# The chosen block's heads with values as the standing operand, and late weight loads one behind each routed tile

## The chip, the cores and the metric

The kernel runs on one core of a Trainium2 chip. The metric is device time in microseconds (us) of one execution. The engines are named as the profile names them: PE multiplies matrices (PEld loads its weights), DVE and ACT do element-wise work, POOL is GpSimd, SP issues DMAs. All arithmetic is fp32; in the trace every fp32 matmul shows as two records.

## The reference, cut to what matters

The input is 2 x 2048 tokens of 256 features. Two layers follow each other. Layer 0 adds a causal attention (one head of 256) and a mixture of 8 experts (each token goes to its two best experts, and two shared experts see all tokens). Layer 1 adds another causal attention and a second feed-forward part that treats only the 255 best-scored tokens of each 2048, the "chosen block":

```python
hn = rmsnorm(x_sel, ln1)                       # 255 chosen tokens
q, kk = rope(heads(hn @ wq)), rope(heads(hn @ wk))
v = heads(hn @ wv)                             # 16 heads of 16
sc = einsum('bhqd,bhkd->bhqk', q, kk) / 4 + m_sel
a = softmax(sc)
o = einsum('bhqk,bhkd->bqhd', a, v).reshape(b, kc, d) @ wo
x1 = x_sel + o
x2 = x1 + gelu(rmsnorm(x1, ln2) @ w1) @ w2     # w1: 256 x 1024
```

The change touches two places: how `einsum(a, v)` of the chosen block is formed, and when weights for later stages are loaded during the routed experts.

## The kernel before, in words

Four stages follow each other on PE. First layer 0's attention (to about 355 us). Then the routed experts (about 355 to 736 us): `for t in range(LIKELY)` runs 36 tiles of 256 sorted tokens, each by `run(t)`. A tile loads the three weights of its expert (`rw`, 512 KB each) and the biases on SP's queue (line 682, 686; two buffers each), fetches its tokens by a transposing DMA (L691), makes fp32 of them on POOL (L696), multiplies gate and up (L703), applies Silu on ACT (L711), multiplies with up on DVE (L712), multiplies down (L718), adds the bias on DVE (L723) and stores (L724). Third the shared experts (L1312, L1331), and fourth layer 1's attention (scores L251, values L316, and L1361 for its queries).

Work that is not in the main chain stands in generators in a list, `side`; `beside()` advances them by a credit after each piece of main work. `chosen_block(b)` is such a generator. For the first half of the tokens (b = 0) its heads run beside the shared experts, about 1059 to 1145 us, and its feed-forward part to 1175 us; for the second half (b = 1) it runs beside layer 1's attention, its heads about 1370 to 1452 us. A scheduler then orders the instructions of each engine's queue, so that the place in a queue differs from the place in the text.

The 16 heads of the chosen block are treated in pairs `h`, and the 256 queries in halves `r`: 16 units for each b. A unit passes three functions, one step apart, so that three units are under way:

- `weigh(h, r)`: queries of the two heads masked on DVE (L1152), two 256-column matmuls for the scores (L1157), scale and mask on DVE (L1162), the maximum (L1167), Exp on ACT with the row's sum (L1170), the reciprocal of the sum (L1173).
- `cross`: four 128 x 128 transposes of the softmax rows on PE (L1179), evacuated to `prT` by DVE or ACT in turn (L150, L152).
- `gather`: four matmuls (L1191) with a 128 x 128 block of `prT` as the standing weights and 16 columns of values `vs` moving; DVE multiplies by the reciprocal into `o` (L1195).

After the 16 units, `o` is transposed (L995), multiplied with `f_wo` (L1222), added to x (L1226), normalised (`rmsnorm`, L1007 to L1015), transposed again and passed to the feed-forward matmuls (L1237) with Gelu on ACT (L1242). These PSUM results all use one tag, `mm`, of two banks.

The late weights are those that the shared experts and layer 1 need. `later_weights()` (L637) issues 17 loads in one go on ACT's queue: eight of 256 KB, six of 512 KB, and three small ones. In the text it is called after tile 18. `layer1_products` multiplies four of them with each other after tile 24 (eight 256-column matmuls).

Of the kernel before, what the change touches and what calls it, by code (L numbers as in the profile page):

```python
# [9 lines left out]
F32 = mybir.dt.float32  # L10
# [3 lines left out]
AF = mybir.ActivationFunctionType  # L14
# [3 lines left out]
P = 128  # L18
# [28 lines left out]
def transformer_kernel(ctx: ExitStack, tc: tile.TileContext, a: dict, out: bass.AP):  # L47
# [15 lines left out]
    def bank(tag):  # L63
        return psum.tile([P, 512], F32, tag=tag, name=f"ps_{tag}")
# [81 lines left out]
    def evacuate(dst, src):  # L146

        copies[0] += 1
        if copies[0] % 2:
            nc.vector.tensor_copy(dst, src)  # L150
        else:
            nc.scalar.copy(dst, src)  # L152
# [17 lines left out]
    def weight(pool, name, tag, queue=None, cols=None):  # L170

        k, n = a[name].shape
        t = pool.tile([P, k // P, cols or n], F32, tag=tag, name=tag)
        (queue or nc.scalar).dma_start(t[:, :, :n], a[name].rearrange("(c p) n -> p c n", p=P))
        return t
# [461 lines left out]
    def later_weights():  # L637

        for n in ("f_wq", "f_wk", "f_wv", "f_wo"):
            fw[n] = weight(w1pool, n, n)  # L640
        for n in ("wq1", "wk1", "wv1", "wo1T"):
            raw[n] = weight(raw_pool, n, n)
        nc.scalar.dma_start(wvo[:, :, D:], a["router_w"].rearrange("(c p) n -> p c n", p=P))
        for n in range(2):
            for name, k in (("sw1", 2), ("sw2", 2), ("sw3", 4)):
                w[name, n] = shared_pool.tile([P, k, 2 * H // k], F32, tag=f"{name}{n}", name=f"{name}{n}")
                nc.scalar.dma_start(w[name, n], a[name][n].rearrange("(c p) n -> p c n", p=P))
        for k, name in enumerate(("sb1", "sb2")):
            w[name] = shared_pool.tile([P, 8], F32, tag=name, name=name)
            nc.scalar.dma_start(w[name], a[name])  # L650

    def layer1_products(after):

# [16 lines left out]
    with ExitStack() as moe:  # L670
        hp = moe.enter_context(tc.tile_pool(name="routed", bufs=2))

        def run(t):
# [24 lines left out]
            for h in range(0, 4, 2):  # L698
                p1, p2 = bank("sc"), bank("tr")
                for ps, we_in in ((p1, w1), (p2, w2)):  # L700
                    for k in range(2):
                        for dc in range(2):
                            nc.tensor.matmul(  # L703
                                ps[:, k * TT : (k + 1) * TT],
                                lhsT=we_in[:, dc, (h + k) * P : (h + k + 1) * P], rhs=xT[:, dc, :],
                                start=(dc == 0), stop=(dc == 1),
                            )
                for k in range(2):
                    act = hp.tile([P, TT], F32, tag="act", name="act", bufs=3)
                    at, hc = slice(k * TT, (k + 1) * TT), slice(h + k, h + k + 1)  # L710
                    nc.scalar.activation(act, p1[:, at], AF.Silu, bias=b1[:, hc])  # L711
                    nc.vector.scalar_tensor_tensor(  # L712
                        hid[:, h + k, :], p2[:, at], b2[:, hc], act, op0=ALU.add, op1=ALU.mult
                    )
# [7 lines left out]
            y = hp.tile([P, 2, D], F32, tag="y", name="y", bufs=3)  # L722
            nc.vector.tensor_tensor(y, po, b3.unsqueeze(1).to_broadcast([P, 2, D]), ALU.add)  # L723
            nc.sync.dma_start(sorted_y[part, :].rearrange("(r p) d -> p r d", p=P), y)  # L724
            return product

        for t in range(LIKELY):
            product = run(t)
            if t == LIKELY // 2:
                later_weights()  # L730
            if t == LIKELY // 2 + 6:
                layer1_products(product)
        used = nc.values_load(filled[0:1, 0:1], min_val=0, max_val=NT)
        with tc.If(used > LIKELY):
            for t in range(LIKELY, NT):
# [237 lines left out]
    def chosen_block(b, fp):  # L973
# [164 lines left out]
        nc.vector.memset(mask[:, :, TOPK - 1 :], -3.0e38)  # L1138
        yield

        o = fp.tile([P, 2, D], F32, tag="hn", name="o")
        queries = {}

        def weigh(h, r):

            dc = h // 8
            if r == 0:

                queries[h] = fp.tile([P, 2, TOPK], F32, tag="qm", name="qm", bufs=2)
                for k in range(2):  # L1150
                    m = (h + k) % 8
                    nc.vector.tensor_scalar(  # L1152
                        queries[h][:, k, :], qkT[:, dc, :], head_of[:, m : m + 1], None, op0=ALU.mult
                    )
            ps = bank("mm")
            for k in range(2):
                nc.tensor.matmul(  # L1157
                    ps[:, k * TOPK : (k + 1) * TOPK], lhsT=queries[h][:, k, r * P : (r + 1) * P],
                    rhs=qkT[:, 2 + dc, :], start=True, stop=True,
                )  # L1160
            pr = fp.tile([P, 2, TOPK], F32, tag="pr", name="pr", bufs=2)
            nc.vector.scalar_tensor_tensor(  # L1162
                pr, ps.rearrange("p (k n) -> p k n", k=2), 0.25,
                mask[:, r, :].unsqueeze(1).to_broadcast([P, 2, TOPK]), op0=ALU.mult, op1=ALU.add,
            )
            nmx = small.tile([P, 2], F32, tag="f_nmx", name="f_nmx")
            nc.vector.tensor_reduce(nmx, pr, AX.X, ALU.max, negate=True)  # L1167
            total = small.tile([P, 2], F32, tag="f_total", name="f_total")
            for k in range(2):
                nc.scalar.activation(  # L1170
                    pr[:, k, :], pr[:, k, :], AF.Exp, bias=nmx[:, k : k + 1], accum_out=total[:, k : k + 1]
                )
            nc.vector.reciprocal(total, total)  # L1173
            return h, r, pr, total

        def cross(h, r, pr, total):
            ps = bank("mm")
            for k in range(4):
                nc.tensor.transpose(  # L1179
                    ps[:, k * P : (k + 1) * P], pr[:, k // 2, (k % 2) * P : (k % 2 + 1) * P], ident  # L1180
                )
            prT = fp.tile([P, 512], F32, tag="prT", name="prT", bufs=2)
            evacuate(prT, ps)
            return h, r, prT, total

        def gather(h, r, prT, total):
            po = bank("mm")
            for k in range(2):
                for c in range(2):
                    at = (2 * k + c) * P  # L1190
                    nc.tensor.matmul(  # L1191
                        po[:, k * HD : (k + 1) * HD], lhsT=prT[:, at : at + P],
                        rhs=vs[:, c, (h + k) * HD : (h + k + 1) * HD], start=(c == 0), stop=(c == 1),
                    )
            nc.vector.tensor_tensor(  # L1195
                o[:, r, h * HD : (h + 2) * HD].rearrange("p (k d) -> p k d", k=2),
                po[:, : 2 * HD].rearrange("p (k d) -> p k d", k=2),
                total.unsqueeze(2).to_broadcast([P, 2, HD]),
                ALU.mult,
            )  # L1200


        first = second = None
# [8 lines left out]
            first = weigh(*unit) if unit else None  # L1212
            yield

        oT = fp.tile([P, 2, TOPK], F32, tag="hT", name="oT")
        transposed(o, oT)
        yield
        x1 = fp.tile([P, 2, D], F32, tag="x1", name="x1")
        for r in range(2):
# [225 lines left out]
```

## Time and profile before

| what | value |
|---|---|
| median of 3 runs | 1566.82 us (1565.46 to 1573.57) |
| profiled execution | 1565.43 us |
| its span in the trace, and mean granted clock | 1563.7 us, 0.984 |
| PE busy, share of the span | 1485.9 us, 95% |
| DVE, ACT, POOL busy | 693.1, 449.5, 408.4 us |
| DMA moved | 183.51 MB, mean 117 GB/s |

PE is busy for 95% of the span; the other engines for less than half. The profiled execution lies 1.4 us below the median, and 1.7 us above its own span. Every duration in this document up to the result is of this execution.

### The profile page before, as it was taken

The page shows a single profiled execution, that of the slowest core. Times are in us where ns is not written, and L with a number is a line of the kernel's source. Part 1 is how long each engine was busy: PE and PEld are TensorE (multiplying, and loading weights), DVE is VectorE, ACT ScalarE, POOL GpSimd, SP SyncE. Part 2 cuts the span into 40 slices and gives each one's busy share as a digit, 9 for nine tenths or more (in the row PEclk, how much of TensorE's full clock was granted, in tenths as well). Part 3 has the DMA queues.
Part 4 walks back from the last instruction along what each step waited for, and adds up shares of the span by engine and source line. Part 5 has one row for each costly group of instructions (what it writes and reads, how often), then busy time and mean ns, then how long its engine had stood idle before and what let it go on. Part 6 is the DMA issues. An engine that isn't in the chain of part 4 may idle for free.

```text
span 1563.7 us, 18180 instructions
## 1 busy us (share of the span) xinstructions
PE 1485.9 (95%) x5956; PEld 1059.9 (68%) x5956; DVE 693.1 (44%) x2067; ACT 449.5 (29%) x838; POOL 408.4 (26%) x594
## 2 busy tenths in 40 slices
PE   6999899997999999999999999999989998998998
PEld 4666566666888888888556556566665765676665
DVE  6346333341222222222234446766545468665354
ACT  2443333331111111111121221125624433343233
POOL 3555577531111111110111111122003123411132
PEclk9999999999999999999999999999999999998999
DMA  5844665669878888674010110220005435521144
GB/s 158 252 112 106 152 135 135 154 127 244 238 219 214 216 216 215 197 207 127 28 41 27 41 41 31 70 90 27 1 10 114 104 75 121 130 49 22 28 118 101
DMA packets 290559, 183.51 MB, mean 117 GB/s; under 512 B 192960, under 2 KB 265408, under 8 KB 290464
## 3 DMA queue, kind: packets, MB, share of 16 engines
q1 hardware_dynamic: 255168, 134.95, 35.5%
q10 hardware_dynamic: 27664, 26.53, 5.8%
q0 software_dynamic: 7632, 20.86, 4.3%
q8 instruction: 48, 0.79, 0.2%
q14 instruction: 47, 0.39, 0.1%
HBM read 93.14 MB, written 45.14 MB: 88 GB/s over the span
## 4 chain that ended last, share of the span: by engine, by line
PE 32%; issue 9%; DVE 6%; POOL 3%; DMA 2%; ACT 1%; POOLq 0%; ACTq 0%; DVEq 0%
PE ps_tr L1312 6%; PE ps_sc L1312 6%; PE ps_pv L1331 5%; POOL planes L301 3%; PE ps_mm L1191 2%; PE ps_mm L1157 2%; PE ps_pv L316 2%; DMA across<-planes 1%; PE ps_sc L251 1%; DVE x L1342 1%; PE ps_mm L1237 1%; PE ps_mm L1179 1%; PE ps_tr L251 1%; PE ps_mm L794 1%; PE ps_mm L1249 1%
## 5 line engine op out<-in xcount | busy, mean ns | idle before, releaser
L301 POOL COPY planes<-row 128x512 uint16<-128x512 uint16 (+3 forms) x320 | 167.5, 568 | 313.6 <-ACT row L270 300.9
L282 ACT COPY pT<-across 128x512 uint16<-128x512 uint16 (+3 forms) x160 | 106.1, 677 | 222.9 <-DMA across<-planes 212.6
L251 PE MATMUL ps_sc<-xnT,qT 128*128 128x512 f32 (+3 forms) x384 | 161.4, 541 | 1.4 <-ACT qT L152 1.2
L712 DVE SCALAR_TENSOR_TENSOR hid<-ps_tr,be,act 128x256 f32<-128x256 f32 x144 | 63.1, 480 | 204.1 <-PE ps_tr L703 187.8
L711 ACT ACTIVATE act<-ps_sc,be 128x256 f32<-128x256 f32 x144 | 60.4, 471 | 310.0 <-PE ps_sc L703 294.1
L1301 POOL DMA_INDIRECT ya<-sorted_y,place x64 | 62.2, 972 | 320.7 <-DVE x L1342 221.3
L718 PE MATMUL ps_pv<-rw,hid 128*128 128x256 f32 x576 | 134.1, 386 | 5.8 <-DVE hid L712 5.8
L316 PE MATMUL ps_pv<-vg,pT 128*128 128x256 f32 x544 | 126.1, 384 | 13.1 <-ACT pT L282 12.7
L703 PE MATMUL ps_sc<-xT,rw 128*128 128x256 f32 x576 | 136.2, 379 | 1.6 <-POOL xT L696 1.6
L703 PE MATMUL ps_tr<-xT,rw 128*128 128x256 f32 x576 | 136.1, 379 | 0.0
L316 PE MATMUL ps_pv<-v,pT 128*128 128x256 f32 x544 | 128.6, 382 | 5.2 <-ACT pT L282 4.1
L696 POOL COPY xT<-xs 128x512 uint16<-128x512 uint16 x72 | 51.5, 762 | 307.5 <-issue 273.1
L316 PEld LDWEIGHTS ps_pv<-vg,pT 128*128 128x128 f32 x544 | 102.6, 191 | 37.5 <-ACT pT L282 18.2
L718 PEld LDWEIGHTS ps_pv<-rw,hid 128*128 128x128 f32 x576 | 106.2, 192 | 27.9 <-DVE hid L712 12.9
L1312 PE MATMUL ps_tr<-xnT,sw 128*128 128x512 f32 x256 | 122.4, 594 | 0.0
L1312 PE MATMUL ps_sc<-xnT,sw 128*128 128x512 f32 x256 | 122.1, 596 | 0.1
L703 PEld LDWEIGHTS ps_sc<-xT,rw 128*128 128x128 f32 x576 | 109.4, 190 | 16.8 <-POOL xT L696 2.0
L703 PEld LDWEIGHTS ps_tr<-xT,rw 128*128 128x128 f32 x576 | 109.4, 190 | 14.9
L316 PEld LDWEIGHTS ps_pv<-v,pT 128*128 128x128 f32 x544 | 101.0, 189 | 27.1 <-ACT pT L282 8.1
L1331 PE MATMUL ps_pv<-sw,hid 128*128 128x256 f32 x512 | 118.6, 381 | 0.0
L1331 PEld LDWEIGHTS ps_pv<-sw,hid 128*128 128x128 f32 x512 | 95.9, 190 | 18.0 <-issue 5.7
L281 DVE COPY pT<-across 128x512 uint16<-128x512 uint16 (+3 forms) x160 | 69.0, 437 | 85.0 <-DMA across<-planes 84.3
(316 smaller groups left out, 1964.9 us busy)
## 6 DMA issues: line engine op xcount, KB each, us to landing
rw<-in_rw SPq DMA_DIRECT2D x108, 512.0 KB, 4.4
sorted_x<-zero ACTq DMA_DIRECT2D x13, 768.0 KB, 6.6
sorted_y<-y SPq DMA_DIRECT2D x36, 256.0 KB, 5.0
be<-biases SPq DMA_DIRECT2D x36, 132.0 KB, 4.5
table<-xn SPq DMA_DIRECT2D x8, 514.0 KB, 3.5
x<-in_x SPq DMA_DIRECT2D x8, 512.0 KB, 6.7
gains<-zero ACTq DMA_DIRECT2D x8, 512.0 KB, 3.2
gain<-gains SPq DMA_DIRECT2D x16, 256.0 KB, 2.7
```

Of the source, the lines that this page charges most:

```text
L251: product = nc.tensor.matmul(ps[:, :w], lhsT=qT[:, dc, (i % 4) * P : (i % 4 + 1) * P], rhs=xnT[g0 + k][:, dc, :w], start=(dc == 0), stop=( ...
L281: nc.vector.tensor_copy(words[:, :, 1], flat[:, :w]),
L282: nc.scalar.copy(words[:, :, 0], flat[:, w : 2 * w]),
L301: nc.gpsimd.tensor_copy(planes[:, h * w : (h + 1) * w], halves[:, :, 1 - h])
L316: product = nc.tensor.matmul(pv[:, :D], lhsT=turned[k][:, j : j + P], rhs=values[g0 + k][:, j // P, :D], start=(c + j == 0), stop=(c + j = ...
L703: nc.tensor.matmul(ps[:, k * TT : (k + 1) * TT], lhsT=we_in[:, dc, (h + k) * P : (h + k + 1) * P], rhs=xT[:, dc, :], start=(dc == 0), stop ...
L711: nc.scalar.activation(act, p1[:, at], AF.Silu, bias=b1[:, hc])
L712: nc.vector.scalar_tensor_tensor(hid[:, h + k, :], p2[:, at], b2[:, hc], act, op0=ALU.add, op1=ALU.mult)
L718: product = nc.tensor.matmul(po[:, r, :], lhsT=hid[:, hc, r * P : (r + 1) * P], rhs=w3[:, hc, :], start=(hc == 0), stop=(hc == 3),)
L1301: nc.gpsimd.indirect_dma_start(out=ya, out_offset=None, in_=sorted_y, in_offset=bass.IndirectOffsetOnAxis(ap=place[rank][:, t : t + 1], ax ...
L1312: product = nc.tensor.matmul(ps, lhsT=ww[:, dc, hc * P : (hc + 1) * P], rhs=xnT[g][:, dc, :], start=(dc == 0), stop=(dc == 1),)
L1331: product = nc.tensor.matmul(po[:, :D], lhsT=hid[:, hc, j * P : (j + 1) * P], rhs=w["sw3", n][:, hc, :], start=(hc == 0), stop=(hc == 3),)
```

## The change

It has two parts that do not touch each other.

In the heads, `gather` does nothing for `r == 0` and works once for each pair of heads, over all 256 queries. The values of one head are copied by DVE into a field of zeros, `apart`, at a fixed place; a 128-column window of it, shifted by the head's place, is the standing operand, so that the head's 16 columns stand at their own rows of the result and the rest is zero. The softmax rows, kept for both halves in `wide`, move as 256 columns. Four such matmuls (2 heads x 2 blocks of keys) accumulate in one bank, and DVE adds the bank to `oT`, which is thereby already transposed. The sums are kept for all heads, and the normalisation is made once at the end: one reciprocal, a copy that spreads each sum over 16 columns, four transposes, and one product.

In the routed experts, `later_weights` becomes a generator that names one load at a time; from tile 12 on, one load is issued behind each tile, with an order dependency on the tile's last Silu. `layer1_products` moves from tile 24 to tile 28.

```diff
     def later_weights():
         for n in ("f_wq", "f_wk", "f_wv", "f_wo"):
-            fw[n] = weight(w1pool, n, n)
+            fw[n] = w1pool.tile([P, 2, D], F32, tag=n, name=n)
+            yield fw[n], a[n].rearrange("(c p) n -> p c n", p=P)
...
-                    nc.scalar.activation(act, p1[:, at], AF.Silu, bias=b1[:, hc])
+                    activated = nc.scalar.activation(act, p1[:, at], AF.Silu, bias=b1[:, hc])
...
+        coming = later_weights()
         for t in range(LIKELY):
-            product = run(t)
-            if t == LIKELY // 2:
-                later_weights()
-            if t == LIKELY // 2 + 6:
+            product, activated = run(t)
+            if t >= LIKELY // 3:
+                for dst, src in (next(coming, (None, None)),):
+                    if dst is not None:
+                        i = nc.scalar.dma_start(dst, src)
+                        tc.add_manual_dep(i.ins, activated.ins.name, order, reason="behind a tile")
+            if t == LIKELY - 8:
                 layer1_products(product)
...
-        o = fp.tile([P, 2, D], F32, tag="hn", name="o")
+        wide = fp.tile([P, 2, 2, 2, TOPK], F32, tag="big", name="wide")
+        gap = P - HD
+        apart = fp.tile([P, 2, 2, 2 * gap + HD], F32, tag="apart", name="apart")
+        nc.gpsimd.memset(apart, 0.0)
+        total = fp.tile([P, 2, HEADS], F32, tag="total", name="total")
+        oT = fp.tile([P, 2, TOPK], F32, tag="hn", name="oT")
...
-            nc.vector.reciprocal(total, total)
-            return h, r, pr, total
+            return h, r, pr
...
-            evacuate(prT, ps)
-            return h, r, prT, total
+            evacuate(
+                wide[:, h // 2 % 2, :, :, r * P : (r + 1) * P], ps.rearrange("p (k c n) -> p k c n", k=2, c=2)
+            )
+            return h, r
-        def gather(h, r, prT, total):
+        def gather(h, r):
+            if r == 0:
+                return
+            dc, at = h // 8, h % 8 * HD
             po = bank("mm")
             for k in range(2):
+                nc.vector.tensor_copy(apart[:, k, :, gap : gap + HD], vs[:, :, (h + k) * HD : (h + k + 1) * HD])
                 for c in range(2):
-                    at = (2 * k + c) * P
+                    lo = gap - at - k * HD
                     nc.tensor.matmul(
-                        po[:, k * HD : (k + 1) * HD], lhsT=prT[:, at : at + P],
-                        rhs=vs[:, c, (h + k) * HD : (h + k + 1) * HD], start=(c == 0), stop=(c == 1),
+                        po[:, :TOPK], lhsT=apart[:, k, c, lo : lo + P], rhs=wide[:, h // 2 % 2, k, c, :],
+                        start=(k + c == 0), stop=(k + c == 2),
                     )
-            nc.vector.tensor_tensor(
-                o[:, r, h * HD : (h + 2) * HD].rearrange("p (k d) -> p k d", k=2),
-                po[:, : 2 * HD].rearrange("p (k d) -> p k d", k=2),
-                total.unsqueeze(2).to_broadcast([P, 2, HD]),
-                ALU.mult,
-            )
+            if at == 0:
+                nc.vector.tensor_copy(oT[:, dc, :], po[:, :TOPK])
+            else:
+                nc.vector.tensor_add(oT[:, dc, :], po[:, :TOPK], oT[:, dc, :])
...
-        oT = fp.tile([P, 2, TOPK], F32, tag="hT", name="oT")
-        transposed(o, oT)
+        nc.vector.reciprocal(total, total)
+        sums = fp.tile([P, 2, D], F32, tag="hT", name="sums")
+        nc.vector.tensor_copy(
+            sums.rearrange("p r (h n) -> p r h n", n=HD), total.unsqueeze(3).to_broadcast([P, 2, HEADS, HD])
+        )
+        ps = bank("mm")
+        for dc in range(2):
+            for r in range(2):
+                at = (2 * dc + r) * P
+                nc.tensor.transpose(ps[:, at : at + P], sums[:, r, dc * P : (dc + 1) * P], ident)
+        nc.vector.tensor_tensor(oT, ps.rearrange("p (c n) -> p c n", c=2), oT, ALU.mult)
```

In the built program the change also alters the order of the queues. ACT's queue before has the 17 loads ahead of and among the Silus of the first routed tiles; after, one load stands behind every fourth Silu from the 52nd on. On PE, the main work's matmuls stand at other places among those of the chosen block: five shared-expert gate and up matmuls of 512 columns (2.5 pairs) stand after the `f_wo` product of b = 0, with 16 down matmuls of 256 columns behind them; and 13 of the attention's value matmuls (L316) stand among the last five head units of b = 1, where before there were none.

## The prediction

> **What bounds the kernel now.** I read the page first, for the engine that fills the span and for the slices in which it doesn't:
>
> ```profile
> span 1563.7 us, 18180 instructions
> PE 1485.9 (95%) x5956; PEld 1059.9 (68%) x5956; DVE 693.1 (44%) x2067; ACT 449.5 (29%) x838; POOL 408.4 (26%) x594
> ...
> PE   6999899997999999999999999999989998998998
> ...
> PEclk9999999999999999999999999999999999998999
> ```
>
> PE bounds it. Each digit is 39 us; a change can gain only by removing PE work, or by filling the few slices below 9. So I asked for busy times by stretch, around the places that the diff touches (columns: length, then PE, PEld, DVE, ACT, POOL busy with counts, clock, DMA share, GB/s):
>
> ```profile
> 376.00:386.00 10.00, 5.38 (x17) 4.50 (x18) 1.57 (x3) 0.84 (x2) 0.00 (x0) 0.66 1.06 365
> 396.00:736.00 340.00, 339.85 (x1568) 293.56 (x1567) 79.40 (x163) 55.31 (x132) 43.04 (x60) 1.00 0.76 207
> 1040.00:1150.00 110.00, 108.86 (x504) 76.31 (x502) 65.83 (x163) 59.32 (x109) 11.85 (x12) 1.00 0.05 15
> 1150.00:1175.00 25.00, 20.50 (x76) 15.60 (x76) 6.70 (x37) 2.39 (x4) 1.97 (x2) 0.86 0.03 11
> 1427.00:1460.00 33.00, 25.64 (x97) 18.06 (x97) 10.69 (x26) 7.81 (x23) 0.00 (x0) 0.69 0.00 1
> ```
>
> Three holes stand out, each with a lowered clock: early in the routed stage, after the heads of b = 0, and in the last head units of b = 1. The rest of the routed stage is full to 0.15 us in 340. PE's waits in those stretches name the causes:
>
> ```profile
> PE ps_pv L718 <- DVE hid L712: 5.7, 1, 5.7
> ...
> PE ps_mm L995 <- DVE hn L1015: 4.6, 1, 4.6
> ...
> PE ps_mm L1179 <- ACT pr L1170: 6.3, 4, 1.6
> ```
>
> **Part B, the late loads.** The scheduler has put the 17 loads at the start of the routed stage, 354.9 to 386 us, not at tile 18. The timeline there:
>
> ```profile
> 371.55 7.93 ACTq L647 DMA_DIRECT2D sw<-in_sw  x2
> ...
> 379.57 0.84 ACT L711 ACTIVATE act<-ps_sc,be 128x256 f32<-128x256 f32 x2 [8.11 <-DMA sw<-in_sw]
> 380.08 0.88 DVE L712 SCALAR_TENSOR_TENSOR hid<-ps_tr,be,act 128x256 f32<-128x256 f32 x2 [8.07 <-ACT act L711]
> ...
> 380.62 4.16 PEld L718 LDWEIGHTS ps_pv<-rw,hid 128*128 128x128 f32 x12 [6.07 <-DVE hid L712]
> 380.62 4.56 PE L718 MATMUL ps_pv<-rw,hid 128*128 128x256 f32 x12 [5.67 <-DVE hid L712]
> ```
>
> ACT sits behind its own DMA issues for 8.11 us; the Silu is late, so `hid` is, so PE stands for 5.67 us. Then twelve records at the lowered clock take 4.56 us; at full clock eight records of this shape take 1.73 us from start to start, 0.216 each, so twelve take 2.6. Loss: 5.7 + (4.6 - 2.6 = 2.0), less about 0.4 for the drained end: 7.3 us.
>
> After the change one issue stands behind a tile's last Silu. An issue takes 0.37 to 0.49 us on ACT, and ACT is idle 2.6 to 6.1 us between its pairs of Silus in the steady stage: nothing, and without that cover at most 17 x 0.45 = 8 us. What else the loads need is DMA time. A tile lasts 10.4 us at a share of 0.76; 512 KB more at the 365 GB/s of the burst are 1.4 us of a tile, raising the share to about 0.9. The stretch from 386 to 396 us ran at 1.13 with PE busy for 10.00 of 10, so SP's `rw` loads (4.4 us to land, double-buffered against 10.4) should keep up; they pass on another queue. Bounds for contention: 0, and, if each of the six 512 KB loads delayed its tile by the 2.6 us by which burst loads grew (`rw` landed in 7.0 there), 16 us. I take 0, by the stretch at 1.13. The eight matmuls of `layer1_products` (8 x 0.43 us) only move by four tiles. **B: -7.3 us.**
>
> **Part A, PE work.** For a pair of heads there were two groups of L1191, eight records each. Undisturbed, a group takes 0.81 to 0.92 us from its start to the next matmul's (1059.14 to 1059.95; 1064.85 to 1065.77), 1.62 to 1.84 for the pair. The new four matmuls of 256 columns have the shape of L703 and L718: 4 x 0.43 = 1.73. Over 16 pairs the difference is between -1.8 and +1.8 us; I take 0.
>
> Here a rule speaks against the change. The Trainium skill, "TensorE: Matmul & The Clock Gate", section "Wait — 56ns, not 53.3ns?", has successive matmuls set apart by their column count alone, with a floor near 25 ns. By it the sixteen narrow records would be 0.4 us and the pair would lose 1.33; sixteen pairs, +21 us. But the row shows 0.10 to 0.115 us for each narrow record: each brings a new 128 x 128 weight, and 16 columns don't hide its load. The same page's "LDWEIGHTS (loading the stationary operand)" gives 107 ns for 128 columns, which fits. I hold to the row.
>
> Four transposes of `o` (L995) are replaced by four of `sums`: 0.
>
> **Part A, other engines.** DVE loses for each pair two L1195 (0.192) and two L1173 (0.162), 0.71 us, and gains two small copies (by the L1195 row, 0.19 each) and one 128x256 add from PSUM (0.42, as L1226): 0.80. DVE is busy 66 of 110 us there: free. At the end of each block it gains a reciprocal (0.17), a 128x512 spread (at most the 0.69 of L1162's shape) and a product (0.69), and two evacuations (0.37 and 0.42) go. Only the product lies between the last gather and `f_wo`; four transposes and two 512-column matmuls (0.43 + 1.7) cover it for b = 0. POOL's clearing of `apart`, about 1 us by its 1.08-us copies of like size, lies many units ahead. New waits: each gather waits for its copies on DVE, whose own operands are old, so they delay only what is behind them on DVE, 0.4 us; PE has `mm` transposes or main work ahead.
>
> **Part A, order.** This is where time comes from.
>
> For b = 0 all shared-expert matmuls are used up at 1148.3 us, just when `rmsnorm` begins on DVE; PE waits 4.6 us for `hn`, 0.6 for `hT`, and then runs four transposes in 1.16 (at full clock 0.43) and L1237 in 9.00 us (32 x 0.216 = 6.9). In the changed queue five 512-column matmuls (5 x 0.86 = 4.3 us) stand between `f_wo` and those transposes, and three of 256 behind them (1.3). The chain from the `f_wo` product to `hn` is 5.1 us, so about 1.0 remains. Saved: 3.6 + 0.6 + 0.7 + 2.1 = 7.0; less half a microsecond for a partial clock: **-6.5 us**.
>
> For b = 1 the main work is used up near 1427. From 1426.7 to 1459.4 us PE does 15.5 us of work at full clock in 32.7: 17.2 us lost. One unit of it:
>
> ```profile
> 1439.21 1.89 PE L1191 MATMUL ps_mm<-vs,prT 128*128 128x16 f32 x8
> 1439.37 0.69 DVE L1162 SCALAR_TENSOR_TENSOR pr<-ps_mm,mask 128x512 f32<-128x512 f32 x1 [2.22 <-PE ps_mm L1157]
> 1441.13 0.19 DVE L1195 TENSOR_TENSOR o<-ps_mm,f_total 128x32 f32<-128x32 f32 x1 [1.08 <-PE ps_mm L1191]
> 1441.24 0.68 DVE L1167 TENSOR_REDUCE f_nmx<-pr 128x2 f32<-128x512 f32 x1
> 1442.01 0.51 ACT L1170 ACTIVATE pr<-pr,f_nmx 128x256 f32<-128x256 f32 x1 [2.86 <-DVE f_nmx L1167]
> ...
> 1442.67 0.69 PE L1179 MATMUL ps_mm<-ident,pr 128*128 128x128 f32 x2 [1.57 <-ACT pr L1170]
> ```
>
> The maximum L1167 is ready at 1440.06 but stands in DVE's queue behind L1195, which waits for the slow gather; Exp and the next transposes follow it. After, in DVE's queue the maximum precedes the gather's add, and 13 attention matmuls (13 x 0.43 = 5.6 us) stand among the last units. The chain mask, maximum, first Exp (0.69 + 0.68 + 0.5 and handovers, 2.2 us) then meets about 2 us of PE work in most units. Left over: about 2 us at the last unit's transposes, 1 at the last gather's evacuation, 1.4 where an attention copy precedes an Exp on ACT, and 2 for the clock, 6.4 in all; and the 13 matmuls, taken from ahead of 1427 where PE was full, shorten that stretch by what they fill here. 17.2 - 6.4 = 10.8; I take **-8.5**, as the move may open small holes earlier (252 us from 1175 had 12 idle).
>
> The 2 us for the clock are a second place where rule and row part: the same page, "HAM oscillation — how this bites in real kernels", warns of PE gaps above 3.4 us; with shorter ones the tail would return to full clock and save 2 more. But in this tail the clock was 0.69 with gaps of 1.57 us, so I keep them.
>
> **Sum.** -7.3 + 0 - 6.5 - 8.5 = -22.3 us on the profiled 1565.4: 1543.1. That execution lies 1.4 below the median of the three; against the median it is **1544.5**. By the bounds (A's PE work ±1.8, b = 0 -4 to -8, b = 1 -4 to -11, contention 0 to +5) 1536 to 1554.
>
> **The rivals.**
> 1. *Only the burst goes.* Main matmuls kept for the two tails are missing earlier, or their transposed tiles are late. For: L316 waits for tiles that a DMA has transposed, and it now stands nearer to them. Against: PE was full where they come from. Then -7.3 alone: 1559.5.
> 2. *The loads merely spread their cost.* `rw` late behind a share of 0.9, PE waiting at L703. For: `rw` landed in 7.0 us in the burst. Against: 10.4 us of cover. A alone: 1552.
> 3. *The wide gather costs (slower).* If the narrow gathers' weight loads were hidden under neighbouring matmuls, each pair would pay 1.33 us more: +21, and with the two tails gained only half (-7) and B -7 still +7 to +21; without these gains 1588. It decides once a pair loses more than 1.4 us (22.3 / 16), counting any wait for its `apart` copies. Against: the 0.81 us measured among full work.
> 4. *It doesn't do what it says*: the loads are drawn together again. ACT's queue shows one behind every fourth Silu, so this is small; then 1552 too.
>
> **How the numbers follow.** About 0.5%, 8 us, is what a measurement of this kernel can tell from no change: faster means below 1559. The sum's case 0.69; rivals 2 and 4 0.07, faster too; rival 1 0.13, half of it on each side of 1559; no effect 0.02; rival 3 0.09. Faster 0.69 + 0.07 + 0.065 = 0.82, same 0.09, slower 0.09. For 8 in 10 the range goes from 1535 to 1561, which takes in the sum's case, rivals 2 and 4 and most of rival 1.
>
> **What would show it.** B right: no wait of L718 near 376 us, ACT's issues one in each of 17 tiles, the routed stage shorter by 7; wrong: waits at L703 from `rw`. A right: gather groups 1.73 us, PE's wait before the second normalisation's transposes about 1 us, clock above 0.85 in the last units of b = 1. Wrong: gathers waiting for DVE's copies, or new PE idle from 1175 to 1427.

## The result and the profile after

The changed kernel takes 1545.3 us in the median of 4 runs (1543.37 to 1547.89), the kernel before 1566.14 us in the median of its 4 (1561.04 to 1573.57). The ratio is 0.9864, 95% interval 0.9822 to 0.9907: faster, by 20.8 us. The forecast was 1544.5.

The profiled execution of the changed kernel took 1543.37 us, the fastest of its four. Its page, first the rows that answer to those shown of before:

```profile
span 1541.7 us, 17887 instructions
PE 1478.2 (96%) x5828; PEld 1050.5 (68%) x5828; DVE 697.3 (45%) x2055; ACT 442.0 (29%) x831; POOL 410.2 (27%) x596
...
PEclk9899999999999999999999999999999999999999
```

PE's busy time has fallen by only 7.7 us, the span by 22.0. So little work went away; idle time and slow clock did. The same stretches of time as before (columns: length, then PE, PEld, DVE, ACT, POOL busy with counts, clock, DMA share, GB/s; the b = 1 heads now end near 1432):

```profile
376.00:386.00 10.00, 10.00 (x48) 8.64 (x47) 2.44 (x5) 1.65 (x4) 1.43 (x2) 1.00 0.79 222
396.00:736.00 340.00, 340.00 (x1569) 293.88 (x1568) 79.83 (x165) 55.25 (x132) 42.85 (x60) 1.00 0.79 219
1150.00:1175.00 25.00, 24.95 (x93) 16.55 (x92) 16.04 (x59) 5.53 (x13) 5.36 (x10) 1.00 0.15 38
1405.00:1440.00 35.00, 31.65 (x139) 22.62 (x138) 19.71 (x55) 12.97 (x34) 3.87 (x8) 1.00 0.13 25
```

The first two holes are closed, and in the third PE is busy for 31.65 of 35 us; the clock is 1.00 in each place. The wait for `hid` (5.7 us) has no successor; no wait of PE above the 0.2 us bound of the list remains from 365 to 735 us. The other two are, in the list of PE's waits:

```profile
PE ps_mm L1192 <- ACT pr L1183: 4.3, 4, 1.8
...
PE ps_mm L1209 <- ACT wide L152: 0.7, 1, 0.7
...
PE ps_mm L1002 <- DVE hn L1022: 0.2, 1, 0.2
```

The wait for the second normalisation fell from 4.6 to 0.2 us, the transposes' wait for Exp from 8.2 us in five waits to 4.3 in four.

To see where the time went I cut both traces at the same instructions: the first gate matmul of the routed stage, the first shared-expert matmul, layer 1's first query product, and the last down product of the b = 1 block. The last two stages are called "shared" and "l1" in what follows, and "rest" is what lies behind.

| kernel | before routed | routed | shared | l1 | rest | span |
|---|---|---|---|---|---|---|
| before | 356.5 | 386.6 | 427.8 | 310.5 | 82.3 | 1563.7 |
| after | 360.1 | 378.6 | 421.8 | 298.8 | 82.4 | 1541.7 |
| difference | +3.6 | -8.0 | -6.0 | -11.7 | +0.1 | -22.0 |

The first column holds the same code in both, and lies between 356.5 and 361.0 us in the profiled executions of all kernels here; its +3.6 is scatter. The next three hold the change.

The stage l1 ends with an instruction of the block, so main work that comes to stand behind the block leaves l1 and enters the rest. Kernels with different orders are therefore compared by the sum of both: 392.8 us before, 381.2 after. PE in that stretch, before and after:

```profile
1170.90:1563.70 392.80, 363.95 (x1479) 250.16 (x1478) 221.92 (x687) 143.48 (x271) 96.47 (x172) 0.97 0.39 86
1160.50:1541.70 381.20, 354.56 (x1415) 241.70 (x1413) 225.98 (x699) 142.37 (x270) 96.91 (x172) 1.00 0.40 88
```

PE's idle time fell by 2.2 us only (28.8 to 26.6). The other 9.4 of the 11.6 us are its own work, done at a higher clock.

### The profile page after: what moved, and what is told of

The parts are those of the page before. It is cut to its first block, busy times and chain, and to the rows that moved or that the text cites. A ratio compares the mean times of both kernels' runs of the same rounds, so it can differ in the third digit from the quotient of the medians.

```text
span 1541.7 us, 17887 instructions
## 1 busy us (share of the span) xinstructions
PE 1478.2 (96%) x5828; PEld 1050.5 (68%) x5828; DVE 697.3 (45%) x2055; ACT 442.0 (29%) x831; POOL 410.2 (27%) x596
## 4 chain that ended last, share of the span: by engine, by line
PE 28%; issue 10%; DVE 7%; POOL 3%; DMA 2%; ACT 2%; SPq 0%; POOLq 0%; ACTq 0%; DVEq 0%
PE ps_tr L1338 6%; PE ps_sc L1338 6%; PE ps_pv L1357 5%; POOL planes L301 3%; DMA across<-planes 2%; PE ps_mm L1209 1%; PE ps_mm L1171 1%; DVE x L1368 1%; PE ps_sc L251 1%; PE ps_mm L801 1%; PE ps_mm L1192 1%; PE ps_pv L316 1%; PE ps_mm L1275 1%; DVE row L262 1%; ACT pr L1183 1%
## 5 line engine op out<-in xcount | busy, mean ns | idle before, releaser
L316 PE MATMUL ps_pv<-vg,pT 128*128 128x256 f32 x544 | 129.0, 390 | 12.4 <-ACT pT L282 12.0
L316 PE MATMUL ps_pv<-v,pT 128*128 128x256 f32 x544 | 128.4, 381 | 7.0 <-ACT pT L282 4.6
L316 PEld LDWEIGHTS ps_pv<-vg,pT 128*128 128x128 f32 x544 | 104.6, 195 | 37.6 <-ACT pT L282 17.5
L316 PEld LDWEIGHTS ps_pv<-v,pT 128*128 128x128 f32 x544 | 101.3, 190 | 29.1 <-ACT pT L282 7.9
```

The lines of the kernel that those rows point to most:

```text
L316: product = nc.tensor.matmul(pv[:, :D], lhsT=turned[k][:, j : j + P], rhs=values[g0 + k][:, j // P, :D], start=(c + j == 0), stop=(c + j = ...
```

## The experiments

Each kernel's stages, from its profiled execution, stand in a table at the end of the section; ratios are to the kernel before. Line numbers of the experiments differ by some lines from those of after; the operand names are the same.

**The two parts apart.** The first takes the hunks of `later_weights` and of the routed loop alone, the second those of the heads alone.

> The kernel before with the late loads alone (part B); the heads are untouched. Stage lengths are taken in the trace, from the first routed gate matmul to the first shared-expert matmul (before 386.6 us, after 378.6). My theory: the burst's hole is all that B removes, so the routed stage is 378.6 +- 0.3, everything behind it as before (427.8 us from the first shared matmul to layer 1's first query product, 310.5 from there to the last down product of the b = 1 block), and the time is about 8 us lower, ratio near 0.995. Rival: part of what the routed stage gains is lost to loads that now compete with the experts' weights; then waits at the gate matmul (L705) show, and the stage is 380 to 384.

> The change with its heads alone (part A); the 17 loads stay in one burst. My theory: the parts add up, so the routed stage is 386.6 as before, with PE's 5.7 us wait for hid, and the two later stages have the lengths of after (421.8 and 298.8): about -18 us in the trace, -14 to -18 in time, ratio 0.988 to 0.991. Rival (the parts lean on each other, for instance because the later weights land at another time): then the later stages are longer than after's by over 1 us.

The loads alone: median 1562.02 us, ratio 0.9962 (0.9945 to 0.9978). That is 4.5 us faster by the medians and 6.0 by the ratio, with an interval from 3.4 to 8.6. The routed stage is 378.6, as in after, and no new wait at the gate matmuls shows. The rival falls. Its profiled execution (1564.33 us) is the second slowest of twelve, and the later stages are 1.5 and 2.0 us longer in it than before. The heads alone: 1553.32 us, ratio 0.9909 (0.9887 to 0.9930). Shared is 421.6, as in after. But routed is 384.3 (in this execution the burst cost 5.7 us, not 8), and l1 is 304.2, 5.4 above after, which is what the rival asked for. Its waits for Exp are those of after (4.4 us in four); the difference is the clock, in the heads-only kernel at the end of the heads of b = 1:

```profile
1430.00:1435.00 5.00, 3.61 (x18) 2.52 (x16) 3.18 (x7) 1.26 (x5) 0.00 (x0) 1.00 0.00 0
1435.00:1440.00 5.00, 3.79 (x11) 2.64 (x12) 0.78 (x2) 1.50 (x5) 0.00 (x0) 0.62 0.00 0
1440.00:1445.00 5.00, 5.00 (x14) 2.84 (x13) 1.81 (x3) 0.00 (x0) 0.00 (x0) 0.70 0.01 3
```

From layer 1's first query product to the end PE's 1414 records stand in the same order in this kernel, in after and in the one with the burst at tile 18 (below). The stretch took 388.3, 381.2 and 379.1 us, with PE idle for 26.2, 26.6 and 25.0: the clock held in two executions and fell in one. So 9 us between the l1 and rest of two single executions can be scatter, and the medians have to decide. The parts add up within their intervals (-4.5 and -13.2 of -20.8); that they lean on each other isn't shown.

**Cover, or the gather's form?** Two kernels raise the credit of the side work, one with the old gather and the late loads, one with the new gather:

```diff
-BESIDE_L0, BESIDE_SHARED, BESIDE_L1 = (2.0, 1.2, 0.72), (0.5, 1.85), 1.25
+BESIDE_L0, BESIDE_SHARED, BESIDE_L1 = (2.0, 1.2, 0.72), (0.5, 1.95), 1.4
```

> Late loads as after, but the old narrow gather; instead the credit by which side work advances is raised (BESIDE_SHARED 1.85 to 1.95, BESIDE_L1 1.25 to 1.4), so that both blocks begin earlier and main matmuls last beyond them: 4.3 us of them between f_wo and the second normalisation's transposes for b = 0, and 2 to 3 us in every one of the last eight head units of b = 1. My theory (A's gain is the order, not the gather's form): the two holes close with the old gather as well; the later stages come within 2 us of after's 421.8 and 298.8, in all -20 to -26 us, ratio 0.984 to 0.988. Rival (the gain is the gather's: less DVE work in the chain of a unit, normalisation taken out of it): the b = 1 hole stays at half or more of its 17 us, and the ratio is 0.990 to 0.995.

> The changed kernel with the same raised credit as in the run with the old gather. My theory: after has only about 3 us of waits left in its last head units, so there is little to win, and early units of b = 1 now stand without main matmuls between them: within 3 us of after to either side, ratio 0.984 to 0.989 to the kernel before. If the gather's form were what counts, it would beat the old gather with the same credit by 8 us or more; by my theory the two are within 3 us of each other.

Measured 1553.16 us, ratio 0.9909 (0.9886 to 0.9932), and 1547.31 us, 0.9880 (0.9856 to 0.9904). The old gather missed its expectation. In l1 its waits for Exp did fall, from 8.4 us to 1.4. But much of the 294.3 us for the stage is work moved behind it (in the rest PE is busy for 84.2 of 94.4 us, with the loads alone for 72.7 of 82.4), and PE waits at the block's first transposes, probably because the higher credit starts the block before its tokens are there. It is the longest of PE's waits in that stage:

```profile
PE ps_mm L1002 <- POOL planes L301: 9.4, 1, 9.4
```

In shared it reached 425.8 instead of 421.8, with 3.0 us still waited for `hn` although the cover stood there. The new gather with this credit had the same loss behind (7.9 us at L1002, rest 98.2). For l1 and rest together the two forms come out equal, 388.7 and 388.3 us; in shared the new one leads by 5.9. The runs mix credit and cover, and didn't settle the question.

So cover was moved by itself. The first kernel has the old gather and keeps value matmuls for the last units; the second is after with its value matmuls held behind the heads. Both add an order dependency in `average`, behind a mark that `gather` (or the transposes of `sums`) leaves:

```diff
+                    if len(marks) == 16 and held_back[0] < 20:      # old gather: three to a unit
+                        unit = min(9 + held_back[0] // 3, 14)
+                        tc.add_manual_dep(product.ins, marks[unit], order, reason="kept for the last heads")
+                        held_back[0] += 1
...
+                    if marks and held_back[0] < 40:                 # new gather: all behind the heads
+                        tc.add_manual_dep(product.ins, marks[0], order, reason="kept behind the heads")
+                        held_back[0] += 1
```

> Late loads as after and the old narrow gather, credits as before; 18 of layer 1's value matmuls (L316), which in the kernel before stand among the middle head units of b = 1 or behind them, are held back by order dependencies to stand three to each of the last head units (1.3 us each). Compared with the run that has the late loads alone, where the l1 stage (layer 1's first query product to the last down product of b = 1) is 312.5 us, the waits for Exp in it are 8.4 us and the granted clock falls to 0.50 from 1432 us. Theory cover: main matmuls between the units shorten the idle stretches and keep the clock, whatever the gather's form; waits for Exp fall below 5 us, the clock in the last five units is 0.9 or more, and the stage is 301 to 306 us. Theory form: 16 columns on a freshly loaded 128 x 128 weight leave PE's array nearly idle, which is what lets the clock fall; then the clock still falls below 0.8 in the last units and the stage is 308 us or more.

> The changed kernel, with the value matmuls that the scheduler had put among the last head units of b = 1 held behind the heads by order dependencies (they then stand between f_wo and the second normalisation). After has 298.8 us in the l1 stage, with a clock of 1.00 in its last units. Theory cover: the hole of before comes back although the gather is wide: waits for Exp of 1.5 us at each of the last four units, the clock below 0.8 there, the stage 306 to 311 us. Theory form: the wide gather keeps the array busy enough; the waits come back but the clock stays at 0.95 or more, and the stage is 300 to 304 us.

The old gather with cover: l1 is 304.1 us instead of 312.5, inside what cover predicts, though its waits for Exp (5.4 us in eight) are a little above the 5 us expected; its last two stretches of heads (PE busy 4.47 and 4.04 of 5 us) run at full clock, where the kernel with the late loads alone had 0.50:

```profile
1432.00:1437.00 5.00, 4.47 (x29) 3.46 (x28) 2.89 (x7) 1.09 (x4) 0.00 (x0) 1.00 0.00 0
1437.00:1442.00 5.00, 4.04 (x25) 2.91 (x25) 1.14 (x4) 1.68 (x5) 0.00 (x0) 1.00 0.01 2
```

Its profiled execution (1553.77 us) is a fast one of ten; the median is 1558.46, ratio 0.9947 (0.9923 to 0.9971), only 3.6 us below the loads alone, with ranges that overlap. For the old gather cover alone gained little time. The new gather without cover: 1558.72 us, ratio 0.9944 (0.9916 to 0.9973), 13 us slower than after with the same operations. Its l1 is 306.4, the waits for Exp are back, 8.6 us in five, and so is the low clock:

```profile
PE ps_mm L1196 <- ACT pr L1187: 8.6, 5, 2.4
...
1425.00:1430.00 5.00, 1.91 (x8) 1.12 (x7) 2.58 (x5) 1.68 (x5) 0.00 (x0) 0.92 0.00 0
1430.00:1435.00 5.00, 5.00 (x17) 3.57 (x17) 1.12 (x2) 0.00 (x0) 0.00 (x0) 0.74 0.00 0
```

With the gather's form fixed, taking the cover away gives back 7.6 us in l1, and the rest grows by 6.6 us, since the held matmuls are late for the attention behind. The sum, 395.4 us, is that of the loads alone (394.9). That the wide gather keeps the clock up by itself is refuted. An early maximum in DVE's queue isn't enough either. In this unit mask, maximum and first Exp follow each other at once, and PE still waits, since it has nothing to do between the scores and their transposes:

```profile
1414.92 1.13 PE L1175 MATMUL ps_mm<-qkT,qm 128*128 128x256 f32 x4
...
1416.18 0.68 DVE L1180 SCALAR_TENSOR_TENSOR pr<-ps_mm,mask 128x512 f32<-128x512 f32 x1
1416.89 0.69 DVE L1185 TENSOR_REDUCE f_nmx<-pr 128x2 f32<-128x512 f32 x1
...
1417.68 0.51 ACT L1187 ACTIVATE pr<-pr,f_nmx 128x256 f32<-128x256 f32 x1
...
1418.33 0.44 PE L1196 MATMUL ps_mm<-ident,pr 128*128 128x128 f32 x2 [2.28 <-ACT pr L1187]
```

A third kernel fills the old gather's waits with idle matmuls, ordered between a unit's scores and its transposes:

```diff
+                for k in range(4):
+                    i = nc.tensor.matmul(
+                        spare[:, :D], lhsT=qkT[:, 0, :P], rhs=vs[:, 0, :], start=(k == 0), stop=(k == 3))
```

> Late loads as after and the old narrow gather; in each of the last five head units of b = 1 four idle 256-column matmuls (1.73 us, result unused) stand between the scores and the next transposes. That adds 5 x 1.73 = 8.6 us of PE work and no cover by useful work. Theory cover: the filling lies in waits that are there anyway (8.4 us) and keeps the clock at 1.00, so the l1 stage becomes shorter than the 312.5 us of the run with the late loads alone: 303 to 308. Theory form: the clock falls all the same, and the stage is 312 us or more.

Its l1 is 307.6, as cover predicts, but the rest is 90.7: 398.3 together, against 394.9 for the loads alone. Of 8.6 us of added work 5.2 were hidden. The spare bank also moved the main matmuls, and the clock fell earlier, at 1415 us (0.58). Time: 1566.33 us, ratio 0.9995 (0.9975 to 1.0014). As a test of cover it is inconclusive, and as a remedy it is none.

**Why the burst costs.** After, with all loads behind tile 18:

```diff
-            if t >= LIKELY // 3:
-                for dst, src in (next(coming, (None, None)),):
+            if t == LIKELY // 2:
+                for dst, src in coming:
```

> The changed kernel with its heads, but all 17 late loads in one row behind tile 18's last Silu, where the text of the kernel before has them, instead of one behind each tile. On ACT's queue each load from the second on waits for an earlier DMA's completion. Theory queue: ACT stands behind its own loads until most have landed (about 5 MB at 365 GB/s, 14 us), so the next tile's Silu is late: one hole at about 550 us, PE waits for hid 5 to 12 us, the routed stage 384 to 392 us instead of 378.6. Rival (the hole of before belongs to the start of the stage, where the experts' first weights and the attention's last transposes also load): at tile 18 the burst is hidden, and the stage is 379 to 381 us.

1557.81 us, ratio 0.9944 (0.9917 to 0.9971), the routed stage 393.6 us: 15 more than after, above the range. In the timeline:

```profile
562.73 5.23 ACTq L734 DMA_DIRECT2D sw<-in_sw  x6
...
569.62 2.68 ACTq L734 DMA_DIRECT2D sb<-in_sb  x2
572.40 1.57 ACT L713 ACTIVATE act<-ps_sc,be 128x256 f32<-128x256 f32 x4 [21.95 <-DMA sw<-in_sw]
...
573.34 1.19 PE L705 MATMUL ps_sc<-xT,rw 128*128 128x256 f32 x2 [11.63 <-issue]
```

ACT gives no Silu for 21.95 us, because most loads of the row wait for an earlier transfer to land, one of the row or one of SP's, and the Silus stand behind them. PE stops when both banks of `ps_sc` are full of gates that no Silu has read: 11.63 us, and then a low clock. The rival is refuted: the burst costs more in the middle than at the start, where a part of it lay before the first tile.

**The order within a step.** In the loop over units the three functions were named in another order, nothing else:

```diff
-            if second:
-                gather(*second)
-            second = cross(*first) if first else None
-            first = weigh(*unit) if unit else None
+            asked = weigh(*unit) if unit else None
+            turned = cross(*first) if first else None
+            if second:
+                gather(*second)
+            second, first = turned, asked
```

> Late loads as after and the old narrow gather; the only edit to the heads is the order in which a step names its three functions: weigh, cross, gather instead of gather, cross, weigh. In DVE's queue the scale of a gather (L1195 of before) then stands behind the next unit's maximum instead of ahead of it, and main matmuls come to stand between the units to the end of both blocks (4.3 us of them behind f_wo of b = 0). If the scale's place in DVE's queue and the cover make up the gain, the stage from the first shared matmul to layer 1's first query product falls from about 428.5 us to 421 to 424 and the l1 stage from 312.5 to 299 to 304, in all -12 to -20 us to the run with the late loads alone, ratio 0.984 to 0.989. If the wide form is needed, less than half of that comes, ratio 0.991 to 0.996.

> The changed kernel with the credit of side work beside the shared experts raised from 1.85 to 1.95, that of layer 1 unchanged: in the run where both were raised the shared stage was 1.9 us shorter than after's, and the loss came later, from a wait of 7.9 us that layer 1's credit brought. Expected: shared stage 419.9, l1 stage and rest as after (298.8 and 82.4), some 2 us faster than after, which a timed comparison can hardly tell (ratio 0.984 to 0.987). Rival: what is won before layer 1 comes back as a wait behind it, and the sum equals after's.

> The changed kernel with the step's order weigh, cross, gather. In its queue most of layer 1's value matmuls again stand ahead of the last three head units of b = 1, with 1.3 us left behind them. By the theory of cover the last units lose their cover and the clock falls there: l1 stage 301 to 306 us, slower than after by 3 to 7 us, ratio 0.987 to 0.991, though no operation is added. If cover were not the cause, it equals after within 2 us.

The old gather with this order takes 1537.22 us, ratio 0.9813 (0.9781 to 0.9844): faster than the change, without its heads (the two were not timed side by side, but after's fastest run is 1543.37 and the slowest here 1538.56). It beat its expectation. Shared is 420.2 with no wait of PE in the list from the first scores on; l1 is 293.6, with one wait for Exp of 1.9 us. One unit of its tail:

```profile
1412.90 1.11 PE L1164 MATMUL ps_mm<-qkT,qm 128*128 128x256 f32 x4
...
1413.09 0.19 DVE L1202 TENSOR_TENSOR o<-ps_mm,f_total 128x32 f32<-128x32 f32 x1 [0.61 <-PE ps_mm L1198]
...
1414.05 0.69 DVE L1169 SCALAR_TENSOR_TENSOR pr<-ps_mm,mask 128x512 f32<-128x512 f32 x1 [0.50 <-PE ps_mm L1164]
...
1414.78 0.69 DVE L1174 TENSOR_REDUCE f_nmx<-pr 128x2 f32<-128x512 f32 x1
1414.80 1.06 PE L1198 MATMUL ps_mm<-vs,prT 128*128 128x16 f32 x8
```

The scale now precedes the mask (I had expected it behind the maximum); between mask and maximum stands only a reciprocal. In the kernel before, the scale of a gather held the maximum back by 1.2 us at half clock (1439.37 mask, 1441.24 maximum) and by 0.8 at full clock (1428.21 and 1429.68). A unit of the tail takes 2.4 to 3.9 us from gather to gather, main work included, instead of 4.4 to 6.2.

But the edit moves a second queue, PE's. Before, the order there was scores, gather, transposes of those scores: 0.8 us of the block's own work stood between a unit's scores and its transposes. Now the transposes of the unit before, a gather and the next scores stand there, 2.1 us.

The changed kernel with the higher credit beside the shared experts only takes 1546.85 us, ratio 0.9874 (0.9843 to 0.9905), no better than after: shared 421.1, l1 302.8. With the new order of the step it takes 1540.65 us, ratio 0.9836 (0.9804 to 0.9867). This expectation failed: I had read from the queue that its last units lose their cover and would be slower, and its median is 4.7 us below after's. Its l1, 289.5 us, is shorter by 9.3, but its rest longer by 6.7. The reading of the queue was wrong: the value matmuls do stand elsewhere, but score matmuls of the attention stand between all of the last units, so cover was there. In this kernel the maximum is held back behind the mask by up to 0.9 us, longer than in after (0.2 at most in the last ten units), and it is faster all the same; so here the gain of the order does not come from an earlier maximum.

The three ran side by side, and the slowest run of the old gather in the new order (1538.56) is below the fastest of the second (1543.47). At the same step order the two forms of the gather are equal in the trace: from the first shared matmul to the end the old one takes 799.1 us, the new one 798.9. Their medians differ by 3.4 us, in favour of the old one, with ranges that overlap.

The last kernel takes value matmuls away from the fast one, by the same order dependency as above:

> The old narrow gather with the step order weigh, cross, gather and the late loads (the run whose l1 stage was 293.6 us, with no Exp wait above 1.9), but the value matmuls that stood among its last head units of b = 1 are held behind the heads. Theory cover alone: without them the last units wait for Exp by about 1.5 us each and the clock falls below 0.8, as in the kernel before: l1 stage 301 us or more, rest of the span about as before, time 8 us or more above the run with cover. Theory chain: with the scale behind the maximum in DVE's queue a unit's own transposes, gather and the next scores (0.43 + 0.83 + 0.87 = 2.1 us) lie beside the 2.2 us from scores to Exp, so the units need no cover: waits under 0.5 us each, clock above 0.9, and the l1 stage with the rest within 4 us of the run with cover (378.9 us in all).

1546.09 us, ratio 0.9854 (0.9811 to 0.9897), 8.9 us above the run with cover. From layer 1's first query product to the last `f_wo` product it takes 270.8 us, as with cover, but for less work: 16 value records fewer, 3.5 us at full clock. Score matmuls, which the edit does not hold, still stand between most of the units, until 1411.06 us; only the last three have nothing between them. PE's rows there:

```profile
1410.90 1.03 PE L1168 MATMUL ps_mm<-qkT,qm 128*128 128x256 f32 x4
1411.76 0.60 PE L1190 MATMUL ps_mm<-ident,pr 128*128 128x128 f32 x4
1412.71 1.07 PE L1202 MATMUL ps_mm<-vs,prT 128*128 128x16 f32 x8 [0.35 <-DVE pr L1173]
1413.62 1.11 PE L1168 MATMUL ps_mm<-qkT,qm 128*128 128x256 f32 x4
1414.57 0.38 PE L1190 MATMUL ps_mm<-ident,pr 128*128 128x128 f32 x2
```

Waits of 0.3 to 0.7 us are left, and a unit with nothing between takes 2.8 us (1411.76 to 1414.57), against 4.4 before at full clock (1426.71 to 1431.11). But the clock falls (0.78 and 0.53 from 1415 to 1425), l1 ends 1.7 later, and the rest is 90.7 instead of 85.3, because the held matmuls delay the attention. Together 386.0 against 378.9: outside the 4 us of the chain theory, while the waits are below what the theory of cover alone expects. The order makes cover matter less, it doesn't replace it.

No run moves PE's queue and DVE's apart. That PE's own order is what the step order gains by is the reading that fits the two wide-gather kernels above (without cover, and with the step order); it isn't shown by itself.

| kernel | routed | shared | l1 | rest | l1 and rest |
|---|---|---|---|---|---|
| loads only | 378.6 | 429.3 | 312.5 | 82.4 | 394.9 |
| heads only | 384.3 | 421.6 | 304.2 | 84.1 | 388.3 |
| old gather, higher credit | 378.7 | 425.8 | 294.3 | 94.4 | 388.7 |
| new gather, higher credit | 378.6 | 419.9 | 290.1 | 98.2 | 388.3 |
| old gather, kept cover | 378.7 | 428.5 | 304.1 | 82.6 | 386.7 |
| new gather, cover removed | 378.7 | 421.7 | 306.4 | 89.0 | 395.4 |
| old gather, filled | 378.6 | 428.9 | 307.6 | 90.7 | 398.3 |
| new gather, burst at 18 | 393.6 | 421.2 | 296.7 | 82.4 | 379.1 |
| old gather, step order | 378.6 | 420.2 | 293.6 | 85.3 | 378.9 |
| new gather, shared credit | 378.6 | 421.1 | 302.8 | 84.4 | 387.2 |
| new gather, step order | 378.7 | 420.3 | 289.5 | 89.1 | 378.6 |
| old gather, step order, no cover | 378.6 | 419.8 | 295.3 | 90.7 | 386.0 |

## Why the prediction was right

**The loads.** -7.3 forecast, -8.0 in the routed stage. Both halves of the step held: the 5.7-us wait and the slow records are gone, and nothing took their place. `rw` lands in 4.6 us in the median (4.4 before); rival 2 is out. The DMA share of about 0.9 that I had worked out for a tile with 512 KB more also holds: over the six tiles with such a load (584.0 to 646.6 us) it is 0.92, with PE busy throughout. Of the wait's cause the prediction had only "its own DMA issues"; the burst at tile 18 shows that it is the waiting of one load for another transfer. In the timed runs the loads alone gave 3.4 to 8.6 us, which takes in 7.3.

**The wide gather's price.** 0 forecast. In the stretch 1042 to 1150 us of before, the 128 narrow records take 13.73 us from start to start, 0.107 each. After:

```profile
1413.13 1.89 PE L1209 MATMUL ps_mm<-wide,apart 128*128 128x256 f32 x8
...
1414.86 0.60 PE L1192 MATMUL ps_mm<-ident,pr 128*128 128x128 f32 x4
```

1414.86 - 1413.13 = 1.73 us for a pair, 13.8 for eight. The rule of a column count with a floor near 25 ns, from the Trainium skill's "TensorE: Matmul & The Clock Gate", section "Wait — 56ns, not 53.3ns?", would have made this +21 us over both blocks. The 0.107 us measured here, with a new weight for each narrow record, decides against it, and rival 3 is out. No wait of PE for DVE's small copies is in the list.

**b = 0.** -6.5 forecast, -6.0 measured; the wait for `hn` is 0.2 where I had left 1.0.

**b = 1.** -8.5 forecast, -11.7 measured in l1, by far the largest difference of the terms, though one within the scatter of single executions. The waits left in the units are 5.0 us (4.3 + 0.7), near the 4.4 that I had listed, and PE's idle time from 1175 to 1405 is 13.6 us, against 12 to 1427 before, so the move opened little. What failed is the 2 us for the clock and the caution beside it: in this execution the clock stayed at 1.00. In the heads-only kernel, with the same queue, it fell at the same place, so the term belongs to some executions and not to others, and the median of after lies 1.9 us above the profiled one. Of the two sides that I weighed, the row's side (keep 2 us) is not refuted. The rule about PE gaps above 3.4 us, from the same page's section "HAM oscillation — how this bites in real kernels", agrees with after, where a gap of 1.84 us left the clock up, but not with before, where no gap just ahead of the fall at 1432 us was above 1.57.

**The mechanism.** I said that the order gives the gain and the gather's form none. Both held: at equal step order the two forms take the same time, and the changed kernel without its cover is 13 us slower. For b = 1 I had named two things, the 13 matmuls as cover and the maximum ahead of the gather's add in DVE's queue. Only the first is borne out: with the value matmuls held behind the heads the maximum is early and PE waits as long as before (8.6 us, and 8.4 with the loads alone). I also took for granted that the order which the scheduler chose needs the rewrite. It doesn't: with the functions of a step named in another order, the old gather is faster than the change. PE's order within a step, which decides how much of the block's own work lies beside the chain through DVE and ACT, was not in the prediction; that it is the cause of that gain is not shown by itself.

The sum met the median within 1 us partly by chance. In the trace +3.6 us before the routed stage, which is scatter, offset 3.2 us that b = 1 gained beyond the forecast; and the medians themselves move by a few us from one set of runs to the next.

## What to carry to other kernels

When a chain leaves the busiest engine and comes back to it, add up the work that stands in that engine's queue between the two places: if it is shorter than the chain, the engine waits. Work of another stage can fill the place, and so can the pipeline's own, if its functions are named in another order. Loads issued from an engine that also computes should be spread behind its work, one at a time. And when a rewrite of the arithmetic changes the time, ask whether it did so through the arithmetic or through the order that the scheduler then chose; the second can often be had without the rewrite.

## What the runs showed of the hardware

The scatter of this kernel goes mostly with the clock of PE. The 30 runs of before beside the cover experiments reach from 1559.0 us at a mean granted clock of 0.988 to 1575.42 us at 0.979; 0.009 of 1567 us is 14 of these 16 us. The three executions with one and the same order of PE's records behind the shared stage show it without a difference in the work: PE's idle time there is within 1.6 us (25.0 to 26.6), its busy time 354.1 and 354.6 us at a clock of 1.00 and 362.1 at 0.98.

Ahead of one fall of the clock stands a stretch of low use, in windows of 4 us of the kernel before:

```profile
1424.00:1428.00 4.00, 4.00 (x25) 3.37 (x24) 2.39 (x7) 1.26 (x5) 0.00 (x0) 1.00 0.00 0
1428.00:1432.00 4.00, 2.13 (x15) 1.76 (x15) 1.64 (x4) 1.51 (x5) 0.00 (x0) 1.00 0.00 0
1432.00:1436.00 4.00, 2.94 (x12) 2.18 (x10) 2.17 (x4) 0.15 (x1) 0.00 (x0) 0.50 0.00 0
```

Four microseconds at 53% busy, without a gap above 1.57 us, are followed by half clock. In after a window with 2.16 of 4 us busy (1424 to 1428) was followed by 3.19 of 4 at a clock of 1.00, and in the heads-only kernel the same order, with waits of 1.83 and 0.68 us, was followed by 0.62. Where the bound lies isn't settled by these runs.
